# A four-layer graph kernel: loading x first, preparing weights inside the first stage, and starting the second stage while the first ends

## The chip, the cores and the metric

The kernel runs on one core of a Trainium2 chip. The metric is the device time of one execution in microseconds, and lower is better. A core has five engines that run their own instruction streams side by side: TensorE (PE in the profile, its weight loads PEld), VectorE (DVE), ScalarE (ACT), GpSimd (POOL) and SyncE (SP, which here only issues DMAs). ACT and POOL can issue DMAs as well.

## The reference

There are 128 graphs of 128 nodes with 128 channels, and an adjacency matrix (0 or 1) for each graph. Four graph layers follow each other; each normalizes its input, applies a Relu, calls its layer and adds the result to x. The two stages that the change touches compute the first layer:

```python
h = jnp.maximum(_layernorm(x, axis=-1), 0.0)
D = jnp.abs(x[:, :, None, :] - x[:, None, :, :])      # x is h here: all pairs of nodes
h = jnp.einsum('bijc,oc->bijo', D, W1) + b1
m = jnp.mean(h, axis=(0, 1, 2))                        # over all graphs and all pairs
v = jnp.mean((h - m) ** 2, axis=(0, 1, 2))
h = _leaky((h - m) / jnp.sqrt(v + EPS) * g1 + be1)
s = jnp.einsum('bijo,uo->biju', h, W2)[..., 0] + b2[0]
A = jax.nn.softmax(jnp.where(A_init > 0, s, NEG), axis=-1)
y = jnp.einsum('bij,bjc->bic', A, x)                   # then Wg, a second normalization, Wt
```

The mean and the variance need every pair of every graph, while the scores are needed only where the adjacency matrix has an edge. Hence the kernel has two stages for this layer: stage 1 makes the statistics over all pairs, stage 2 the attention on the edges.

## The kernel before

**Preparation (lines 185 to 372).** The kernel builds an identity matrix on POOL, loads some thirty weight arrays (matrices on SP's and ACT's queues, columns such as `b1`, `g1`, `qb`, `vb_c` on POOL's), transposes five square matrices on PE, and folds weights for the later layers: `fw`, `w2g`, `aq`, `vpw`, `pb_bc`, `q_avg` and others. Scratch tiles of the pool `wload` hold the raw weights.

**Stage 1, `statistics()` (lines 484 to 700).** Graphs are taken four at a time, 32 groups. `nodes(g)` loads x (`xg`), normalizes it (DVE statistics `ln_s`, `ln_mv`; ACT `ln_rs`; POOL `ln_xn`), stores it to DRAM (`xn_d`), transposes it on PE (`pt`), applies the Relu (`he`), stores it (`h_d`) and makes three bf16 parts `us` of the product with W1 (`pu`). Then `block(b, q)` runs for every graph and each quarter of its pairs: a difference `d` (128 channels by 2048 pairs) on DVE (line 605) or POOL (line 610), its absolute value on ACT (line 614), a product with W1 on PE (line 631, `ph`), and sums on DVE (line 643) or ACT (line 637). Blocks with `is_larger` take a maximum instead of the difference and add three bf16 products with `us` and a constant pattern `both`. A chain of small operations on DVE, PE and POOL then turns the sums into the scale `h_sc` and the offset `h_bi` (lines 658 to 700).

**Stage 2, `edge_attention()` (lines 702 to 1105).** It first forms constants (`off`, `at`, `in_half`, `in_other`, `not_own`, `upto`, `down`, `least`, `room` and others, lines 716 to 758) and the score of a node with itself (`own`, `own_d`). Then it takes the same 32 groups. A group loads the adjacency matrices (`adj`), `xn` and `ht`, casts to bf16 (`adjb`), ranks the edges (`other`, `half`, `rank`, `keys`, `more`, `ranks`, `pos`, `row`, `in_row`) and so forms a matrix `inc` that selects the edges. For each graph PE then forms the differences over edges (`diff`), ACT takes the absolute value (`d`), PE multiplies by W1 (`ph`), ACT applies the statistics (`z`, with `h_sc` and `h_bi`), and further steps make the scores `pl` and the attention. Side steps split h into bf16 parts (`parts`), form values (`values`, `pz`), check the matrix (`check`, `pc`), form the masked base (`bases`, which needs `own_d`) and store x with a bias (`with_bias`, `xb`).

**What sets the order.** Inside each stage the instruction order of PE, ACT, DVE and POOL is written out by a planner, `in_order`. A step is a generator that yields `(engine, planned work in us, slots it takes, slots it frees)`. Among the steps that are ready the planner takes the one that can begin first. Slots stand for buffers (`p` for PSUM banks, `in` for a group's inputs, `d` for differences), and a chain may wait for a named event with `yield "after", ...`. Each call of the planner starts with all engines free at time 0. SP is not in this order. The kernel's third stage (the remaining layers, from line 1106 on) uses the same planner and is not changed. Stage 2's tiles lie in memory that stage 1 or the weight scratch used before, and stage 1's in that of the weight scratch.

## Time and profile before

| what | value |
|---|---|
| time, median of 3 runs | 2709.62 us (2708.36 to 2710.77) |
| profiled execution: time | 2713.54 us |
| profiled execution: span, first to last instruction | 2711.7 us |
| mean granted TensorE clock | 0.966 |
| first x load issued | 21.49 us |
| first pair block on POOL, DVE | 35.58, 36.08 us |
| POOL's last pair block ends | 1079.9 us |
| first load of stage 2 issued | 1090.17 us |
| first selection product (`diff`) of the steady run | 1115.94 us |

A line of a timeline gives the start, the duration, the engine, the source line, the operation, the tile written and the tiles read, the number of instructions merged into it, and in brackets how long the engine had been idle and what released it. In a table of stretches each engine has its busy time and in brackets its number of instructions. A queue name such as SPq is the time in which an engine issues a DMA. Times of PE are modelled at their ends.

### The profile page before, as it was taken

The numbers are of one execution on the slowest core, as the hardware profiler recorded it, in microseconds if no ns is written. First come the engines' busy times: TensorE is split into PE (matmuls) and PEld (weight loads), VectorE is DVE, ScalarE is ACT, GpSimd is POOL, SyncE is SP. The second block draws the span as 40 slices with busy tenths as digits, with TensorE's granted clock in tenths as the row PEclk, the third lists the DMA queues.
The fourth block names the chain that finished last, engine by engine and source line by source line (L and its number), as shares of the span: only waits on it lengthen the run. The fifth ranks groups of instructions, "written<-read, shape, count | busy, mean of one in ns | idle before, by whom it ended". The sixth has DMA issues, their size and how long they took to land. (4 is left out here: it accounts for less than half of the span.)

```text
span 2711.7 us, 51703 instructions
## 1 busy us (share of the span) xinstructions
PE 2497.3 (92%) x19597; PEld 1559.2 (57%) x19597; DVE 2416.1 (89%) x4660; ACT 2161.6 (80%) x3531; POOL 1644.8 (61%) x943
## 2 busy tenths in 40 slices
PE   6999999999999999799999999968988888898888
PEld 3334333434333333577777777756766767667666
DVE  6999999999999998788988888778988888889886
ACT  4999999999999999466566666568787877787885
POOL 7999999999999999635435343022333333333234
PEclk8999999999999999899999999979999999999999
DMA  2000000000000000523222231040211111111001
GB/s 69 16 27 30 24 24 28 24 24 24 24 24 24 24 20 9 161 74 100 81 85 86 78 100 42 17 137 6 62 29 54 36 44 44 41 42 33 9 2 33
DMA packets 134257, 122.62 MB, mean 45 GB/s; under 512 B 9504, under 2 KB 100960, under 8 KB 134000
## 3 DMA queue, kind: packets, MB, share of 16 engines
q1 hardware_dynamic: 131360, 117.83, 14.1%
q8 instruction: 158, 2.59, 0.4%
q10 hardware_dynamic: 2032, 1.31, 0.2%
q14 instruction: 99, 0.81, 0.1%
q0 software_dynamic: 608, 0.07, 0.0%
HBM read 73.05 MB, written 46.14 MB: 44 GB/s over the span
## 5 line engine op out<-in xcount | busy, mean ns | idle before, releaser
L610 POOL TENSOR_TENSOR d<-he 128x2016 f32<-128x2016 f32 (+1 forms) x272 | 959.8, 3559 | 15.0 <-DVE six L643 7.8
L631 PE MATMUL ph<-d,w1T 128*64 128x504 f32 (+1 forms) x4096 | 910.0, 594 | 22.9 <-DVE six L643 13.2
L614 ACT ACTIVATE d<-d 128x2048 f32<-128x2048 f32 (+1 forms) x448 | 832.2, 1888 | 18.1 <-POOL d L610 12.4
L631 PEld LDWEIGHTS ph<-d,w1T 128*64 128x64 f32 x4096 | 320.2, 136 | 545.0 <-issue 459.9
L605 DVE SCALAR_TENSOR_TENSOR d<-pt,he 128x2048 f32<-128x2048 f32 x240 | 541.4, 2269 | 0.7 <-PE ph L631 0.7
L643 DVE BATCH_NORM_STATS2 six<-ph 128x6 f32<-128x512 f32 (+1 forms) x704 | 435.8, 676 | 13.4 <-PE ph L631 12.0
L1568 POOL TENSOR_TENSOR xn<-xo,mv 128x512 f32<-128x512 f32 x64 | 73.9, 1155 | 324.8 <-DVE mv L1561 257.5
L975 PE MATMUL pl<-its,it 128*128 128x128 f32 x1280 | 168.2, 280 | 1.5 <-DVE its L968 1.2
L875 POOL CAST h<-xn 128x512 bf16<-128x512 f32 x32 | 21.5, 672 | 243.5 <-DVE xn L869 229.4
L637 ACT ACTIVATE ph<-ph 128x1008 f32<-128x1008 f32 x160 | 159.7, 998 | 9.8 <-PE ph L631 8.8
L975 PEld LDWEIGHTS pl<-its,it 128*128 128x128 f32 x1280 | 154.4, 193 | 15.0 <-DVE its L968 6.5
L1671 DVE SCALAR_TENSOR_TENSOR p<-z,mask 128x1024 f32<-128x1024 f32 x124 | 147.7, 1210 | 8.3 <-ACT z L1669 8.0
L1569 POOL TENSOR_TENSOR xn<-xn,rs 128x512 f32<-128x512 f32 x96 | 111.1, 1158 | 49.6 <-ACT rs L1565 37.9
L937 ACT ACTIVATE z<-ph,h_bi,h_sc 128x320 f32<-128x320 f32 x128 | 78.5, 617 | 74.5 <-PE ph L934 73.8
L923 PE MATMUL diff<-inc,h 128*128 128x320 bf16 x768 | 130.0, 306 | 2.9 <-DVE inc L843 2.5
L1669 ACT ACTIVATE z<-z 128x1024 f32<-128x1024 f32 x128 | 129.0, 1008 | 4.0
L930 ACT ACTIVATE d<-diff 128x640 f32<-128x640 f32 x128 | 89.8, 702 | 52.9 <-PE diff L923 51.7
L843 DVE SCALAR_TENSOR_TENSOR inc<-in_row,row 128x4 bf16<-128x4 f32 (+12 forms) x512 | 125.5, 315 | 1.2 <-PE in_row L836 1.2
L965 ACT CAST it<-pi 128x640 f32<-128x640 bf16 x128 | 87.0, 689 | 47.3 <-PE pi L962 46.1
L1568 POOL TENSOR_TENSOR xn<-x,mv 128x512 f32<-128x512 f32 x32 | 36.5, 1139 | 138.3 <-DVE mv L1561 65.9
L968 DVE TENSOR_TENSOR its<-pi,s 128x640 f32<-128x640 bf16 x128 | 102.9, 810 | 15.0 <-ACT it L965 14.1
L1700 PE MATMUL va<-p,vals 128*32 128x128 f32 x2048 | 107.8, 283 | 8.0 <-DVE vals L1685 7.8
(349 smaller groups left out, 5349.8 us busy)
## 6 DMA issues: line engine op xcount, KB each, us to landing
ht<-h SPq DMA_DIRECT2D x64, 256.0 KB, 2.8
xg<-in_x SPq DMA_DIRECT2D x32, 256.0 KB, 2.7
n<-ln_xn SPq DMA_DIRECT2D x32, 256.0 KB, 2.4
h<-he SPq DMA_DIRECT2D x32, 256.0 KB, 2.6
adj<-in_adj SPq DMA_DIRECT2D x32, 256.0 KB, 3.1
xn<-n SPq DMA_DIRECT2D x32, 256.0 KB, 2.7
xb<-in_x SPq DMA_DIRECT2D x32, 256.0 KB, 3.3
xb<-xb SPq DMA_DIRECT2D x32, 256.0 KB, 2.0
```

What stands on the lines that cost most here:

```text
L605: nc.vector.scalar_tensor_tensor(dv, own, 0.0, later, ALU.max, ALU.max if is_larger else ALU.subtract)
L610: nc.gpsimd.tensor_tensor(dv, later, own, ALU.subtract)
L614: nc.scalar.activation(d[:, 0 : 4 * n], d[:, 0 : 4 * n], AF.Abs, accum_out=sums[:, g, k : k + 1] if on_act else None,)
L631: nc.tensor.matmul(ph[64 * a : 64 * a + 64, t, 0:n], wt, x_, start=part == 0, stop=not is_larger or part == 3,)
L637: nc.scalar.activation(ph[:, :, 0:n], ph[:, :, 0:n], AF.Square, accum_out=squares[:, g, k : k + 1])
L643: nc.vector.bn_stats(six[g][:, 2 * by_bn.index((i, q)) + t, :], ph[:, t, 0:n])
L843: nc.vector.scalar_tensor_tensor(inc[:, :, e : e + n], in_row[:, :, 0:n], float(k + 1), row[:, :, 0:n], ALU.is_equal, ALU.subtract,)
L923: nc.tensor.matmul(diff[:, a, 0 : SLOT_N // 2], h[:, i, :], inc[:, a * SLOT_N // 2 : (a + 1) * SLOT_N // 2], start=m == 0, stop=m == 2,)
L975: nc.tensor.matmul(made["pl"][:, i, :], it[:, k, :], its[:, k, :], start=k == 0, stop=k == 4)
L1569: nc.gpsimd.tensor_tensor(xn, xn, bcast(rs, 2, P), ALU.mult)
L1669: nc.scalar.activation(z, z, AF.Exp, scale=1.0 - SLOPE)
L1671: nc.vector.scalar_tensor_tensor(p, z, 1.0, bcast(mask[:, i, :], 1, NH), ALU.max, ALU.mult)
```

## The change

The change has three parts.

1. **Start.** The pools for the later inputs, for stage 2's tiles (`mid`) and for the weight scratch are placed on the other side of the memory. The first two groups of x are loaded there at once, the first as SP's first DMA. All columns that POOL loaded go to SP's queue. POOL's two memsets go to DVE.
2. **Weights inside stage 1.** The preparation becomes generators (`first_weight`, `own_and_later`, `attention_weights`, `square_weights`, `edge_constants`) that the planner of stage 1 places among its own steps, with planned waits of 4 to 30 us ahead of them. `both` is added up on POOL instead of DVE. Four of the transposed matrices are copied together. `edge_constants` holds stage 2's constants; `least` is one instruction instead of 16.
3. **Boundary.** `in_order` returns when each engine and slot is free, and stage 2's call starts from these times. The final statistics become the chain `total`, the first maker of stage 2's planner. A step can wait for several events; two new ones are `begun` (the latest of stage 1's engine times) and `stats` (the end of `total`). Stage 2's inputs and first tiles (`adj`, `xn`, `ht`, `adjb`, `half`, `other`, `more`, `ranks`, `row`, `h1` to `h3`) lie in `mid`, which shares no memory with stage 1's tiles. `z` and the second half of `bases` wait for `stats`; `xb`, `zg`, the first half of `bases`, `inc` and the first `d` wait for `begun`. The two statistics products become one.

```diff
-def in_order(makers, most, room, kept):
+def in_order(makers, most, room, kept, begun=None):
-    free_at = dict.fromkeys(AFTER, 0.0)
-    slots = {kind: [0.0] * n for kind, n in room.items()}
-    chains, events = [], {}
+    free_at = dict.fromkeys(AFTER, 0.0) if begun is None else dict(begun)
+    slots = {kind: [0.0] * n if isinstance(n, int) else list(n) for kind, n in room.items()}
+    chains, events = [], {"begun": max(free_at.values())}
...
+    return free_at, slots
...
+    raw_x = [wl.tile([P, GB, P], F32, tag=f"x{g}", name=f"x{g}") for g in range(2)]
+    nc.sync.dma_start(raw_x[0], x_t[:, 0:GB, :])
...
+    raw("w1", w["L0_gnn_W1"], nc.sync)
+    nc.sync.dma_start(raw_x[1], x_t[:, GB : 2 * GB, :])
...
-        nc.gpsimd.dma_start(t[0:n], src)
+        nc.sync.dma_start(t[0:n], src)
...
+    def attention_weights():
+        yield "wait", 5.0
+        yield DVE, 2.9, "", ""
...
+    def square_weights(psum2):
+        yield "wait", 8.0
+        yield PE, 1.3, "ph", ""
...
+        pt = psum2("w_ps").rearrange("p a (b c) -> p (a b) c", c=P)
+        for k, name in enumerate(("wg", "wt0", "wt1", "kw", "pw")):
+            nc.tensor.transpose(pt[:, k, :], raws[name], ident)
+        yield ACT, 0.9, "", "ph"
...
+        yield PE, 1.7, "ph", ""
+        pv = psum2("vw_ps")
+        pvw, pvb = pv[:, 0, 0:P], pv[0:1, 1, 0:P]
+        nc.tensor.matmul(pvw, raws["vw"], pwT, start=True, stop=True)
+        nc.tensor.matmul(pvb, vb_c, pwT, start=True, stop=True)
...
+    def edge_constants():
+        yield "wait", 30.0
+        yield POOL, 0.6, "", ""
+        nc.gpsimd.iota(
...
+            def own_and_later():
+                yield POOL, 3.9, "", ""
+                nc.gpsimd.tensor_tensor(
+                    both.rearrange("p (i j) -> p i j", j=64),
...
+            def first_weight():
+                yield "wait", 4.0
+                yield PE, 0.3, "ph", ""
...
+                if g < len(raw_x):
+                    xg = raw_x[g]
+                    yield "wait", 4.0 + 1.2 * g
...
-            makers = [partial(nodes, 0)]
+            makers = [partial(nodes, 0), others]
...
+                free_at, slots = in_order(
+                    makers, A_UNDER_WAY + 1, {"d": A_D, "ph": 3} | two, A_KEPT
+                )
+        banks = sorted(slots["pt"]) + [at for at in sorted(slots["ph"]) for _ in range(2)]
+
+        def total(psum, done):
+            yield "after", "begun"
+            yield DVE, 1.0, "", ""
...
+            yield "done", "stats"
...
             def bases(g, adjb, made):
+                yield "after", "begun"
                 yield ACT, 0.62, "", ""
                 base = tile_f("base")
                 nc.scalar.activation(base, adjb, AF.Identity, bias=far, scale=-NEG)
+                yield "after", "stats"
                 yield POOL, 2.5, "", ""
...
+                if g == i == 0:
+                    yield "after", "begun"
                 yield ACT, 0.6, "d", "q"
...
+                yield "after", "stats"
                 yield ACT, 0.53, "", "p"
                 z = made["z"][:, i, :]
...
-            makers = [partial(group, g) for g in range(n_parts)]
+            makers = [partial(total, psum, own_d), *(partial(group, g) for g in range(n_parts))]
```

## The prediction

> **What bounds the kernel now.** I read the page's first two parts, then a table of busy time by stage, then the timelines at both places the change touches. Columns of a stage row: stretch, its length, busy time and instruction count of PE, PEld, DVE, ACT, POOL, granted clock, DMA share, GB/s.
>
> ```profile
> span 2711.7 us, 51703 instructions
> PE 2497.3 (92%) x19597; PEld 1559.2 (57%) x19597; DVE 2416.1 (89%) x4660; ACT 2161.6 (80%) x3531; POOL 1644.8 (61%) x943
> ...
> 0.00:36.00 36.00, 14.31 (x56) 9.65 (x56) 16.24 (x71) 7.59 (x21) 18.75 (x36) 0.78 0.40 111
> 36.00:1090.00 1054.00, 1031.78 (x5224) 412.67 (x5224) 1033.63 (x1279) 1025.18 (x1075) 1026.30 (x360) 1.00 0.07 23
> 1090.00:1116.00 26.00, 10.63 (x62) 8.45 (x61) 19.57 (x108) 7.21 (x14) 18.12 (x19) 0.73 0.69 214
> 1116.00:1774.00 658.00, 626.12 (x5428) 484.41 (x5427) 549.18 (x1413) 403.68 (x853) 267.08 (x242) 0.97 0.24 77
> ```
>
> The reader should see four stretches with different limits. In the first 36 us no engine is half busy beyond POOL: weights are prepared and nothing of x is worked on. From 36 to 1090 (stage 1) four engines are all 97 to 98% busy, DVE the fullest: no engine has room for much more. From 1090 to 1116 PE works 10.6 of 26 us, partly at half clock. From 1116 PE carries stage 2 (626 of 658 us).
>
> The timeline of the start and of the boundary (start, duration, engine, line, operation, idle before and its releaser):
>
> ```profile
> 6.88 1.28 ACT L494 ACT_TABLE_LOAD   x1 [6.88 <-DMA a2b<-in_L_gnn_a]
> 21.49 6.49 SPq L525 DMA_DIRECT2D xg<-in_x  x3
> 21.87 2.29 DVE L512 TENSOR_TENSOR both<-ident 128x2048 bf16<-128x2048 f32 x1
> 35.58 42.24 POOL L610 TENSOR_TENSOR d<-he 128x2016 f32<-128x2016 f32 x12
> 36.08 2.28 DVE L605 SCALAR_TENSOR_TENSOR d<-pt,he 128x2048 f32<-128x2048 f32 x1
> ```
>
> ```profile
> 1090.17 0.39 SPq L793 DMA_DIRECT2D adj<-in_adj  x1
> 1093.35 0.61 POOL L802 CAST adjb<-adj 128x512 bf16<-128x512 int32 x1 [13.46 <-DMA adj<-in_adj]
> 1095.22 0.22 DVE L437 SCALAR_TENSOR_TENSOR h_bi<-af_off,h_sc,be 128x1 f32<-128x1 f32 x1
> 1110.73 0.40 PE L836 MATMUL in_row<-row,ranks 128*128 128x128 bf16 x4 [3.71 <-DVE row L832]
> 1115.94 1.49 PE L923 MATMUL diff<-inc,h 128*128 128x320 bf16 x5 [2.47 <-DVE inc L843]
> ```
>
> The first x load is issued only at 21.49, after the last use of the weight scratch, and the first pair block follows 14 us later. At the boundary POOL, done with stage 1 at 1079.9, idles 13.46 us for a load that is issued at 1090.17, when stage 1's memory comes free. The statistics are ready at 1095.2, but PE gets its first diff at 1116: the long chain there is group 0's own (load, adjb, half, rank, row, inc).
>
> **The start, part by part.** x is issued at about 0.7 in place of 21.49 and needs 2.8 us to land, so about 4. Its four statistics took 2.2 us (24.25 to 26.4): 6.2. Next is ACT's rs, behind the table load, which stood at 6.88 because ACT first issues seven DMAs. Those paused: a2b was issued at 3.71, when w1c had landed (0.74 plus 3.0), and araw at 5.55, when Wg had (1.38 plus 4.1): as if some eight transfers could be under way at once. The change puts 19 small DMAs of POOL on SP, so that SP issues 27 (0.37 to 0.59 us each, 10 to 16 us) and with ACT's 34 share that limit: 34 / 8 x 3.5 us is 15 us. So the table load ends between 8.2 (as now) and 15; I take 10.5, nearer the row because ACT's issues are early in each queue. Then rs 0.5, product on POOL 1.04, transposes 1.11, Relu 0.60, copy 0.40 and hand-overs: he is whole at about 14.4. POOL's second normalization (2.1) comes next: its first d at 16.5 instead of 35.58, 19 us earlier. DVE's first d waits for pu and the three us parts (1.8 + 4 x 0.42 and hand-overs): 18.5 instead of 36.08, 17.5 earlier. PE follows at 20.8 instead of 38.42, 17.6 earlier. A DMA store of xn or h behind SP's 27 issues delays no one: its buffer is wanted a group, 33 us, later. SP's late ones are vb_c and pb_row: PE's pvb and DVE's sum wait for them (12 to 16 plus 2.3 us to land), and behind them on PE stands pu of group 0: 0 to 4 us, inside my range.
>
> The forming of "both" moves from DVE (2.29) to POOL; the nearest POOL row is a 2016-element difference at 3.56. It ends near 5 to 6, before POOL's first wanted product at 10.5: it costs nothing. [...]
>
> **What is now inside stage 1.** From the rows before 22 us and at 1095 to 1099, DVE's moved work is: layer 1's attention weights 6.4 (products 0.76 and 0.84, sums 0.74 twice, copies 0.74, ident_far and the small sums 1.9, the rest of it 0.7 and hand-overs), square weights 2.2 (aT 1.08 in it), stage 2's constants 5.4, sign of both and w1T2 0.9: 14.9 us. Some 4 fit before the first d; 11 stand between pair blocks, and the third group's statistics (1.6), formerly before 36, too. Hence DVE nets 17.5 - 12.6 = 5 us. PE has 30 instructions, 7 us, most before its first block: nets 15. POOL loses 2.1 and 0.5 for the iotas: nets 16. ACT loses 2.5: nets 15. If DVE carries the stage strictly, it ends 5 us earlier (0 if the start is at its late bound); if PE does, 15. Against DVE as the only limit: from 1050 to 1089 PE never stopped, and DVE's idle time in the last 20 us of it was about 8, waiting for ph. I take 9, bounds 0 and 16.
>
> **The boundary.** Stage 1 ends on PE at T = 1089.9; the first diff is at T + 26. Now three groups' adj, xn and ht lie in memory of their own, loaded before; POOL goes on at T - 10 with adjb 0.6, other and half 2.75, so rank can run right at T. DVE then has for group 0: keys and more 0.9, ranks, pos, row 3.3, parts 0.8, inc 3.9: 8.9 us, with PE twice between (1 us), and the statistics' DVE steps (7.6 planned; 1088.8 to 1095.2 measured, waits included) woven in; about 3 us of theirs stand in group 0's way. First diff at T + 13: 13 us saved. Bounds: 6, if all statistics go ahead of group 0; 18, if they fall into its gaps. Constants (5.4 on DVE, done at 1099.2) leave this path; they were paid above. New waits: z on ACT, and base plus edge on POOL, wait for the statistics (own_d, some T + 12). Behind z on ACT stand other groups' copies, and ph keeps a bank: but first ph comes about T + 14, so the wait has ended. d of graph 0 and the xb load wait for "begun", which is T + 1: nothing.
>
> PE's clock fell to 0.50 between 1095 and 1105 and again between 1115 and 1120; 24 pz matmuls took 5.41 us there. PE still has gaps in my sum, so I count no gain from it; full clock would give about 3. [...]
>
> **Sum.** 9 + 13 = 22 us from the profiled execution: 2713.54 (span 2711.7, 1.8 around it) gives 2691.5. That execution was 3.9 above the median 2709.62, so I expect 2687.6, say 2688. Within 0.2% (5.4 us) this kernel can't be told from no change.
>
> **Rivals.** *DVE carries all of it.* Late table load and 12.6 us of DVE work eat the start; only the boundary remains, at 6 to 13: 2709.6 - 10 = 2700. For it: DVE is the fullest engine, 98.1%. Against: the PE tail.
> *Both ends do better.* DVE's slack absorbs the inserts (15 to 16) and the boundary gives 18, or a warm clock 3 more: 35 saved, 2675. For it: POOL, ACT and PE all start 17 to 19 earlier.
> *Stage 2 runs worse (the slower side).* Its whole order is planned anew, from unequal free times and with new waits. The place is the 658 us from 1116; PE is busy 95.2% of it. Each point of that share costs 7 us; the 22 us are gone at 626 / 680 = 92.1%, and at 91% (688 us) the time is 2718. For it: the planner's plan doesn't hold on the chip exactly; after 1774 PE is busy only 814.5 of 938. Against: nine groups are under way and PE's waits in stage 2 are single microseconds per line.
> *It doesn't do what it says:* stage 2 loads still wait for stage 1, the start gains 4 to 8: 2703.
>
> **How the numbers follow.** Forecast 0.62 (2678 to 2699), DVE 0.13, better 0.13, worse 0.09, doesn't 0.03. Leaving out the far halves of the outer cases, 8 in 10 is 2673 to 2706. Faster by over 0.2% (under 2704.2): 0.62 + 0.13 + 0.11 + 0.01 = 0.87; within: 0.05; slower: 0.08.
>
> **What would show it.** Right: the first POOL d near 16 and PE's first block near 21; last stage 1 matmul near 1081 (1076 to 1090); first diff 8 to 20 us after it; POOL casts adjb directly after its last d, not after a DMA; stage 2 still about 655 us. Wrong: ACT's table load after 15; PE waiting for vb_c beyond 20; DVE idle under 3 us in the last 40 us of stage 1 (DVE carries); diff still 25 us behind stage 1; PE under 93% in stage 2.

## The result: 28 us slower, and where the time is

Before and after were run side by side, five times each. The changed kernel takes 2737.26 us (2736.23 to 2743.38) and the kernel before 2709.13 us (2708.36 to 2710.77). The ratio is 1.0109, with a 95% interval of 1.0095 to 1.0124. The prediction was 2688. The profiled execution of the changed kernel took 2736.81 us, with a span of 2735.0.

The stages show that the loss and a gain partly cancel. All times are from the two profiled executions, in us.

| place in the profile | before | after | change |
|---|---|---|---|
| first pair block on POOL (`d`) | 35.6 | 37.4 | +1.8 |
| first pair block on DVE (`d`) | 36.1 | 53.9 | +17.8 |
| first stage 1 product on PE (`ph`) | 38.4 | 56.3 | +17.9 |
| last stage 1 product begins | 1089.5 | 1140.5 | +51.0 |
| first `diff` of stage 2 | 1113.0 | 1159.9 | +46.9 |
| last `diff` of stage 2 | 1745.2 | 1770.6 | +25.4 |
| span | 2711.7 | 2735.0 | +23.3 |

So the first 56 us lose 18, the rest of stage 1 loses another 33 (1084.2 us from the first product to the last, 1051.1 before), the boundary gains 4 (19.4 us from the last product to the first diff, 23.5 before), and stage 2 gains 21.5 (610.7 us from the first to the last diff, 632.2 before). What follows the last diff is 2 us shorter. (The ratios are worked out from the single runs, so they can differ a little from the quotient of two medians. The first `diff` of the table is a single product; the steady run begins at 1115.94 before and at 1162.69 after.)

The page of the changed kernel, first part, and then the table of busy time by stretch (columns as in the table of before: PE, PEld, DVE, ACT, POOL, granted clock, DMA share, GB/s):

```profile
span 2735.0 us, 51581 instructions
PE 2485.0 (91%) x19595; PEld 1552.3 (57%) x19595; DVE 2456.2 (90%) x4648; ACT 2159.1 (79%) x3527; POOL 1634.4 (60%) x923
...
0.00:56.00 56.00, 8.97 (x36) 7.28 (x36) 29.31 (x71) 8.55 (x20) 28.53 (x24) 1.00 0.49 139
56.00:1141.00 1085.00, 1041.45 (x5244) 417.85 (x5245) 1052.79 (x1308) 1024.66 (x1075) 1020.63 (x362) 0.99 0.07 22
1141.00:1163.00 22.00, 9.07 (x72) 6.77 (x71) 17.01 (x64) 7.03 (x15) 9.58 (x10) 0.76 0.50 155
1163.00:1799.00 636.00, 614.84 (x5415) 480.12 (x5413) 559.64 (x1415) 399.89 (x849) 261.07 (x241) 0.98 0.24 77
```

DVE is busy 40 us longer over the whole kernel (2456.2 against 2416.1) with 12 instructions fewer, and 19 us longer in stage 1 alone (1052.79 against 1033.63). PE, by contrast, is busy 12 us less (2485.0 against 2497.3). The timeline of the changed kernel's start shows both halves of the loss:

```profile
19.80 0.98 SPq L617 DMA_DIRECT2D xg<-in_x  x2
...
24.29 0.29 DVE L622 BATCH_NORM_STATS2 ln_s<-xg 128x6 f32<-128x128 f32 x1 [13.84 <-DMA xg<-in_x]
...
25.90 0.26 DVE L622 BATCH_NORM_STATS2 ln_s<-x 128x6 f32<-128x128 f32 x1
...
38.24 2.94 DVE L339 COPY w2g<-gw 128x2 f32<-128x2 f32 x1
...
45.18 3.31 DVE L341 TENSOR_SCALAR ident_far<-ident 128x128 bf16<-128x128 f32 x1
...
49.32 2.62 DVE L355 TENSOR_TENSOR parts_m<-of_part 128x1 f32<-128x1 f32 x1
...
53.89 2.22 DVE L700 SCALAR_TENSOR_TENSOR d<-pt,he 128x2048 f32<-128x2048 f32 x1
...
26.06 1.04 POOL L631 TENSOR_TENSOR ln_xn<-xg,ln_mv 128x512 f32<-128x512 f32 x1 [21.07 <-DVE ln_mv L623]
...
37.42 14.49 POOL L705 TENSOR_TENSOR d<-he 128x2016 f32<-128x2016 f32 x4
```

The first half is a wait in DVE's order. The first two groups of x (tile `x`) were issued at 0.74 and 1.87 us, but DVE takes the statistics of the third group (tile `xg`) first. That load is an ordinary one, and SP issues it at 19.80, behind 27 others. DVE stands idle for 13.84 us until it lands, and everything else it has to do, the first two groups' statistics at 25.90 and the weights included, stands behind.

The second half is the duration of small operations. POOL's first four differences begin at 37.42 and, one by one, end at 41.15, 44.91, 48.41 and 51.92. A copy of 128x2 that took 0.16 us before begins at 38.24 and ends at 41.18; `ident_far`, 0.22 us before, ends at 48.49; a sum of two columns, 0.16 us before, ends at 51.94. Each ends just after a POOL difference has ended. Between 31 and 130 us, twelve lines of the weights' preparation with 16 such operations add up to 32.7 us. Where POOL does next to no arithmetic, as in the preparation of the kernel before, the same work takes 3.9 us. The difference is 29 us of DVE time that no plan had. Some 12 of these 29 us stand before DVE's first difference and are part of the late start.

The boundary in the timeline of the changed kernel:

```profile
1125.29 15.77 PE L726 MATMUL ph<-d,w1T 128*64 128x512 f32 x72
1142.32 0.38 PE L886 MATMUL rank<-upto,other 128*128 128x128 bf16 x4 [1.26 <-ACT ph L732]
1143.17 0.69 DVE L893 TENSOR_TENSOR more<-key_row,keys 128x512 bf16<-128x512 f32 x1 [0.21 <-PE key_row L888]
...
1145.90 0.28 PE L776 MATMUL act_m<-all_sums,w1TT 128*128 128x1 f32 x2
...
1150.28 0.68 DVE L899 TENSOR_TENSOR ranks<-rank,half 128x512 bf16<-128x512 f32 x1
...
1152.34 0.56 PE L907 MATMUL in_row<-row,ranks 128*128 128x128 bf16 x4 [0.73 <-DVE row L903]
...
1157.28 0.22 DVE L518 SCALAR_TENSOR_TENSOR h_bi<-af_off,h_sc,be 128x1 f32<-128x1 f32 x1
...
1157.61 1.28 DVE L916 SCALAR_TENSOR_TENSOR inc<-in_row,row 128x512 bf16<-128x512 f32 x2
...
1162.69 1.49 PE L1000 MATMUL diff<-inc,h 128*128 128x320 bf16 x5 [2.40 <-DVE inc L916]
```

The loads are indeed out of the way: `rank` runs 1.3 us after stage 1's last product, which ends at T = 1141.06. But between `more` (done at 1143.9) and `ranks` (1150.28) DVE works on the statistics, and waits 1.76 us in it for their first product, which PE does only after a group of `pz` and `pc`. After `in_row` (done at 1152.9) DVE finishes all the statistics, 1157.5, before it takes `inc`. The steady run of diffs begins at T + 21.6; before it was T + 26.

Stage 2 itself was not expected to move. The kernel before has gaps in it that the changed one does not have. Two stretches of 5 us of before (columns as above), and the matmul in them:

```profile
1305.00:1310.00 5.00, 3.21 (x20) 2.08 (x21) 4.32 (x8) 0.96 (x5) 4.92 (x5) 0.67 0.01 2
1310.00:1315.00 5.00, 5.00 (x39) 3.33 (x38) 2.79 (x5) 3.27 (x8) 0.76 (x2) 0.65 0.79 238
```

```profile
1307.33 1.02 PE L943 MATMUL sp<-w_slide,z 128*128 128x2 f32 x4 [1.79 <-DVE z L448]
```

PE waits 1.79 us for DVE, and the granted clock in these 10 us is 0.67 and 0.65. In narrower stretches it is 0.50 from 1306.7 to 1313.4, where PE is busy 6.07 us. Six `diff` products took 0.99 us at 1302.14, at a clock of 1.00, and 1.78 us at 1309.85, at 0.50; by that ratio some 3 us of work are lost beside the gap, an estimate. The clock falls to 0.50 in the same way near 1487.6 (6.7 us), 1654.9 (3.3) and 1678.8 (3.3). The whole hundreds of microseconds around them have PE busy 95.3 to 98.7 us at a clock of 0.97 to 1.00. In the changed kernel, from 1262 on, each hundred has 98.7 to 99.1 us at 1.00. The waits of PE in stage 2, by cause, fall from 18.5 us to 7.4, and PE's busy time there from 626 to 615 us for the same work. Together that is about the 21 us.

### The profile page after: what moved, and what is told of

Read it like the earlier page. It is cut to its first block, busy times and chain, and to the rows that moved or that the text cites. A ratio compares the mean times of both kernels' runs of the same rounds, so it can differ in the third digit from the quotient of the medians.

```text
span 2735.0 us, 51581 instructions
## 1 busy us (share of the span) xinstructions
PE 2485.0 (91%) x19595; PEld 1552.3 (57%) x19595; DVE 2456.2 (90%) x4648; ACT 2159.1 (79%) x3527; POOL 1634.4 (60%) x923
## 4 chain that ended last, share of the span: by engine, by line
PE 43%; DVE 34%; ACT 12%; issue 6%; POOL 3%; DMA 1%; SPq 0%; DVEq 0%; ACTq 0%; POOLq 0%
PE ph L726 12%; DVE d L700 8%; DVE six L738 6%; ACT d L709 4%; PE pl L1055 4%; PE diff L1000 4%; DVE p L1751 3%; PE ph L1013 2%; POOL d L705 2%; PE sp L1023 2%; PE po L1708 2%; PE va L1780 1%; DVE s L1639 1%; ACT ph L732 1%; PE ph L1910 1%
## 5 line engine op out<-in xcount | busy, mean ns | idle before, releaser
L726 PE MATMUL ph<-d,w1T 128*64 128x512 f32 (+1 forms) x4096 | 914.5, 597 | 43.4 <-DVE six L738 29.8
L709 ACT ACTIVATE d<-d 128x2016 f32<-128x2016 f32 (+1 forms) x448 | 831.0, 1887 | 38.6 <-DVE d L700 23.7
L987 POOL TENSOR_TENSOR base<-base,own_d 128x512 f32<-128x512 f32 x32 | 42.7, 1334 | 177.5 <-PE ph L1013 121.5
L916 DVE SCALAR_TENSOR_TENSOR inc<-in_row,row 128x8 bf16<-128x8 f32 (+12 forms) x512 | 126.5, 315 | 0.8 <-PE in_row L907 0.8
L1996 POOL TENSOR_TENSOR xh<-xh,xo 128x512 f32<-128x512 f32 x32 | 46.9, 1468 | 106.0 <-DVE xh L1717 82.2
```

The source lines that it names most:

```text
L709: nc.scalar.activation(d[:, 0 : 4 * n], d[:, 0 : 4 * n], AF.Abs, accum_out=sums[:, g, k : k + 1] if on_act else None,)
L726: nc.tensor.matmul(ph[64 * a : 64 * a + 64, t, 0:n], wt, x_, start=part == 0, stop=not is_larger or part == 3,)
L916: nc.vector.scalar_tensor_tensor(inc[:, :, e : e + n], in_row[:, :, 0:n], float(k + 1), row[:, :, 0:n], ALU.is_equal, ALU.subtract,)
```

## The experiments

The theory after the result: **(1)** the late third load makes DVE and all behind it start late; **(2)** small DVE operations beside POOL's differences last until the running difference ends; **(3)** stage 2 gains from its new order. Rivals: the loss is the new weight work as such, or the order of stage 1; and stage 2 gains from its own memory, not the order. This table has, from each profiled execution, the start of DVE's first `d`, the time from the first to the last stage 1 product, from there to the first diff, and from the first to the last diff. The ratio is to runs of the kernel before on the same chip, whose medians were 2712.89 (e1 to e4), 2711.6 (e5 to e8) and 2710.02 us (e9 to e11).

| kernel | time, us | ratio, 95% interval | DVE's first `d` | stage 1 | to diff | diffs |
|---|---|---|---|---|---|---|
| before | 2709.13 | 1 | 36.1 | 1051.1 | 23.5 | 632.2 |
| after | 2737.26 | 1.0109 (1.0095 to 1.0124) | 53.9 | 1084.2 | 19.4 | 610.7 |
| e1 three x | 2714.84 | 1.0001 (0.9991 to 1.0011) | 36.1 | 1075.0 | 19.4 | 610.9 |
| e2 three x, weights first | 2689.00 | 0.9909 (0.9893 to 0.9926) | 31.0 | 1054.7 | 19.4 | 611.0 |
| e3 boundary alone | 2690.55 | 0.9909 (0.9893 to 0.9926) | 32.1 | 1054.5 | 19.4 | 612.1 |
| e5 planned from zero | 2706.13 | 0.9975 (0.9966 to 0.9985) | 32.7 | 1051.6 | 23.7 | 623.2 |
| e7 one order | 2698.67 | 0.9957 (0.9940 to 0.9974) | 44.6 | 1051.5 | 19.4 | 610.8 |
| e8 weights, then pairs | 2704.73 | 0.9979 (0.9968 to 0.9989) | 35.3 | 1070.7 | 19.5 | 611.7 |
| e9 the same, one order | 2695.35 | 0.9948 (0.9931 to 0.9964) | 26.0 | 1069.1 | 19.4 | 613.0 |
| e10 order alone | 2703.02 | 0.9972 (0.9961 to 0.9982) | 38.2 | 1050.5 | 23.7 | 619.4 |
| e11 two x, weights first | 2715.96 | 1.0024 (1.0014 to 1.0033) | 37.9 | 1074.4 | 19.5 | 613.3 |

### e1: a third group of x loaded early

```diff
-    raw_x = [wl.tile([P, GB, P], F32, tag=f"x{g}", name=f"x{g}") for g in range(2)]
+    raw_x = [wl.tile([P, GB, P], F32, tag=f"x{g}", name=f"x{g}") for g in range(3)]
...
-    nc.sync.dma_start(raw_x[1], x_t[:, GB : 2 * GB, :])
+    for g in (1, 2):
+        nc.sync.dma_start(raw_x[g], x_t[:, g * GB : g * GB + GB, :])
```

> Edit: the changed kernel with a third group of x in the early loads, so that DVE's first statistics no longer stand behind an x load that SP issues after 24 small ones. Theory A (DVE's head-of-line wait until 24.3 us cost about 18 us of the start, the rest is lost elsewhere): POOL's first pair block near 18 to 22 us in place of 37.4, time 2737 - 15 to 20 = about 2719. Rival B (the weight steps on DVE set the start and the wait lies beside them): POOL's block moves, but DVE's first pair block and the time do not, 2733 to 2739.

Measured: 2714.84 us, 22 below the changed kernel, with DVE's first difference at 36.1; POOL's came at 27.9 and not at 18 to 22. In the profile the last stage 1 product comes 27 us earlier, 18 of them from the start and 9 from the stage, and what follows the last diff took 6 us longer in this execution. Set against the kernel before on its own chip, the difference is 26. The late load is worth 22 to 27 us by itself. What remains above the boundary's gain is stage 1, still 24 us longer than before's. In it DVE is idle for almost nothing in the first 100 us; the small operations fill it: those that begin after DVE's first difference take 23 us. From the groups of DVE by shape between 36 and 130 us of e1 (count, busy us, mean ns, idle before):

```profile
L397 DVE COPY aT<-araw 128x256 f32<-128x256 f32 x4 | 4.6, 1148 | 0.0
L437 DVE TENSOR_SCALAR back<-at 128x128 f32<-128x128 f32 x1 | 3.6, 3637 | 0.0
L438 DVE TENSOR_TENSOR tmp<-back,ident 128x128 f32<-128x128 f32 x1 | 3.5, 3534 | 0.0
```

Other lines are hit than in the changed kernel (there `back` took 1.2 us and `tmp` 1.1), as is to be expected if chance decides at what point of a POOL difference an operation begins. The trace of e1 also shows the wait that the prediction put at 0 to 4 us: PE stands 8.11 us before `pvb`, until 23.07, for `vb_c`, with the first group's `pu` behind it.

### e2: the same, and the weights ahead of everything

```diff
-                if g == 0:
-                    yield "after", "w1"
-                    yield "after", "both"
...
-            makers = [partial(nodes, 0), others]
+            makers = [partial(nodes, 0)]
...
+            for gen in (own_and_later(), first_weight(), attention_weights(), square_weights(psum2), edge_constants()):
+                for _ in gen:
+                    pass
             with tc.manual_schedule(engines=ORDERED):
...
-                    makers, A_UNDER_WAY + 1, {"d": A_D, "ph": 3} | two, A_KEPT
+                    makers, A_UNDER_WAY, {"d": A_D, "ph": 3} | two, A_KEPT
```

The chain of the weights no longer counts among those under way, so their number goes down by one.

> Edit: as the first run, and all weight and constant steps taken out of the planner's order, ahead of stage 1. Theory C (DVE copies and scalar operations that run beside a POOL pair block last 1 to 3.6 us instead of 0.2, about 30 us in all, and this is what moving them into stage 1 cost): no weight operation over 1.3 us, last pair product of stage 1 near 1085, time 2685 to 2695. Rival D (their own length is the cost, 11 us, wherever they stand): 2705 to 2712.

Measured: 2689.00 us, 26 below e1, 0.9% below the kernel before and 1.8% below the changed one. No weight operation stands in stage 1, and the stage is back to 1054.7 us. DVE even begins its pair blocks 5 us earlier than in e1, because the same operations are short while POOL has no pair blocks (`a1bc` and the scaling of `pb_row` took 3.32 and 3.08 us in e1, 0.73 and 0.31 here).

### e3: the boundary and stage 2 alone

The weights stand ahead of stage 1 as in e2, all 19 column loads are on POOL's queue again, and no x is loaded early.

```diff
-    raw_x = [wl.tile([P, GB, P], F32, tag=f"x{g}", name=f"x{g}") for g in range(2)]
+    raw_x = [wl.tile([P, GB, P], F32, tag=f"x{g}", name=f"x{g}") for g in range(0)]
...
-    nc.sync.dma_start(raw_x[1], x_t[:, GB : 2 * GB, :])
...
-        nc.sync.dma_start(t[0:n], src)
+        nc.gpsimd.dma_start(t[0:n], src)
```

> Edit: the changed boundary and second stage, but weights prepared ahead of stage 1, columns loaded by POOL as before, and no x load ahead of the weights. If the boundary and the newly planned stage 2 are worth what the profile of the changed kernel shows (4 us to the first diff, 21 us inside stage 2), and stage 1 starts and runs as before or a little earlier: 2680 to 2688. If stage 2 was only faster because stage 1 ended late or left something done: 2700 to 2710.

Measured: 2690.55 us, just above the range for the gain standing by itself. The first product on PE comes 4 us earlier than in the kernel before (x no longer shares memory with the weight scratch). The rest of the gain is the boundary (4) and stage 2 (20), less 3 in stage 1. So the early x, which was the first part of the change, is worth next to nothing against e3: e2, which has three early groups, is 1.6 us below it, within the spread.

### e4: small operations in stage 1 of the kernel before

```diff
+            def probe(k):
+                yield DVE, 0.3, "", ""
+                kind = k % 4
+                if kind == 0:
+                    nc.vector.tensor_copy(pr_a, ident)
+                elif kind == 1:
+                    nc.vector.scalar_tensor_tensor(pr_b, ident, 1.0, ident_h, ALU.mult, ALU.max)
+                elif kind == 2:
+                    nc.vector.tensor_reduce(pr_c, ident, AX.X, ALU.add)
+                else:
+                    nc.vector.tensor_scalar(pr_b, ident, 2.0, None, ALU.mult)
...
+                if 4 <= b < 124:
+                    makers.append(partial(probe, b))
```

> Edit: the kernel before, with 120 small DVE operations on 128x128 in stage 1, 30 each of: copy f32 to bf16, scalar_tensor_tensor with two inputs, reduction, scalar operation f32 to f32. They add work that nothing uses. Theory C: copies and scalar operations last 1.5 to 2 us on average beside POOL's pair blocks (each waits for the running one), with single values up to 3.6; the reduction and the two-input operation 0.3 to 0.4; the time grows by 80 to 130 us. Rival D: all four last 0.2 to 0.4, time at most 40 us longer.

Measured: one time of 2892.01 us, 179 above the kernel before and so more than the 80 to 130 of theory C. The groups of DVE by shape:

```profile
L656 DVE SCALAR_TENSOR_TENSOR pr_b<-ident,ident_h 128x128 f32<-128x128 f32 x30 | 76.9, 2562 | 0.0
L660 DVE TENSOR_SCALAR pr_b<-ident 128x128 f32<-128x128 f32 x30 | 55.7, 1857 | 0.0
L654 DVE CAST pr_a<-ident 128x128 bf16<-128x128 f32 x30 | 44.8, 1493 | 0.0
L658 DVE TENSOR_REDUCE pr_c<-ident 128x1 f32<-128x128 f32 x30 | 7.9, 265 | 0.0
```

120 operations that the plan held to be 0.3 us each take 185 us, and the time grows by 179: in stage 1, DVE time is time. The sums stay at 0.265 us, the other three kinds do not. That the two-input kind would stay short was wrong: it was the longest.

### e5: the boundary alone, but planned from zero

```diff
-                    makers, B_GROUPS, {"p": banks[0:6], "q": banks[6:7], "in": B_IN, "w": B_W, "d": 3, "it": 3, "ge": 1, "eT": 2, "yt": 2, "xb": 2}, {"p": 1}, free_at
+                    makers, B_GROUPS, {"p": 6, "q": 1, "in": B_IN, "w": B_W, "d": 3, "it": 3, "ge": 1, "eT": 2, "yt": 2, "xb": 2}, {"p": 1}
```

> The kernel of the boundary alone, with stage 2's planner called as before the change: every engine and slot free at time 0. Memory, tiles, constants, loads and the chain of the statistics stay as changed. Theory A (the 21 us of stage 2 come from the new order, since the planner now knows when each engine comes free): the stretch from the first to the last diff goes back from 611 to about 632 us, PE again shows gaps of 1 to 2 us with a granted clock near 0.6 behind each, and the time is 2690.5 + 21 = 2711. Theory B (they come from the memory of their own and the loads made ahead, not from the order): the stretch stays at 609 to 615 and the time within 5 us of 2690.5.

Measured: 2706.13 us, between the theories. The diffs take 623.2 us, 11 of the 21 are back, and the boundary is 23.7 us as in the kernel before. The waits of PE and its clock come back too (100 us stretches at 0.95 to 1.00). So with the other parts in place, knowing when each engine comes free is worth about 16 us in all: 4 at the boundary and 11 in stage 2. The rest of stage 2's gain needs something else as well; see e10.

### e6: what lengthens a small operation

A call of `round_of` runs the eight kinds on DVE, with 2 to 8 sums after each; the copy of `last` makes the second set wait until POOL is done.

```diff
+            for r in range(14):
+                round_of(r, True)
+            for _ in range(115):
+                nc.gpsimd.tensor_tensor(big_o, big_a, big_b, ALU.subtract)
...
+            nc.vector.tensor_copy(last, big_o[:, 0:1])
+            for r in range(14):
+                round_of(r, True)
```

> The kernel before, with a stretch put ahead of stage 1 whose results nothing uses: POOL runs 115 differences of 128x2016 (3.56 us each) while DVE runs eight kinds of small operations on 128x128, 14 of each, with 2 to 8 small sums between them; then DVE runs the same list again with POOL idle. Theory A (a DVE operation that reads and writes SBUF, whatever its number of inputs, waits for POOL's running operation; one that reads PSUM, a sum and a memset do not): in the first stretch copy, one-input and two-input kinds have means of 1 to 2.5 us and none above about 3.9, the PSUM kinds, sums and memsets stay at 0.17 to 0.45; in the second stretch all stay at 0.16 to 0.45. Theory B (any DVE operation beside POOL is slowed by a share): all kinds are longer in the first stretch by the same factor. Theory C (the lengthening has to do with stage 1's other work on ACT and PE, not with POOL): no kind is longer in the first stretch. The time is some 600 to 900 us above before's; nothing is read from it.

Groups of DVE by shape while POOL works:

```profile
L1130 DVE TENSOR_REDUCE o_sum<-src 128x1 f32<-128x128 f32 x560 | 158.8, 284 | 15.5
L1116 DVE TENSOR_TENSOR o_two<-src,ident 128x128 f32<-128x128 f32 x14 | 44.5, 3176 | 0.0
L1115 DVE TENSOR_SCALAR o_one<-src 128x128 f32<-128x128 f32 x14 | 43.5, 3106 | 0.0
L1114 DVE COPY o_copy<-src 128x128 f32<-128x128 f32 x14 | 34.2, 2443 | 0.0
L1120 DVE TENSOR_SCALAR o_h<-src_h 128x128 bf16<-128x128 bf16 x14 | 31.8, 2270 | 0.0
L1117 DVE SCALAR_TENSOR_TENSOR o_ps<-ps_in,src 128x128 f32<-128x128 f32 x14 | 3.9, 281 | 0.0
L1122 DVE SCALAR_TENSOR_TENSOR o_max<-ps_in,ident 128x128 f32<-128x128 f32 x14 | 3.9, 281 | 0.0
```

and the same list with POOL idle:

```profile
L1130 DVE TENSOR_REDUCE o_sum<-src 128x1 f32<-128x128 f32 x560 | 159.2, 284 | 15.5
L1116 DVE TENSOR_TENSOR o_two<-src,ident 128x128 f32<-128x128 f32 x14 | 3.9, 282 | 0.0
L1117 DVE SCALAR_TENSOR_TENSOR o_ps<-ps_in,src 128x128 f32<-128x128 f32 x14 | 3.9, 281 | 0.0
L1114 DVE COPY o_copy<-src 128x128 f32<-128x128 f32 x14 | 3.0, 217 | 0.0
L1115 DVE TENSOR_SCALAR o_one<-src 128x128 f32<-128x128 f32 x14 | 3.0, 216 | 0.0
```

Theory A holds, with longer means than it named. Copies, one-input and two-input operations between tiles in SBUF go from 0.18 to 0.28 us up to means of 2.27 to 3.18 us, the longest 4.38, which is about the length of one POOL operation here (4.43 us; 3.56 in stage 1; why the two differ was not tested). Operations that read PSUM (0.281 us), memsets (0.165) and sums over a row (0.284) do not change at all. POOL's own 115 operations all last 4.42 to 4.46 us, whether DVE works beside them or has already finished its first set. PE and ACT had nothing to do in either stretch, which excludes theory C. Stage 1's own DVE work consists of the kinds that are spared: `d` (2.27 to 2.28 us in every trace here) and the operations that make `us` (0.41) read PSUM, and the rest are statistics, which in the kernel before last as long beside POOL's differences as with POOL idle (`six` 0.68 and 0.69 us, `ln_s` 0.26 in both). That is why stage 1 of the kernel before shows nothing of this, and why the weights, most of them SBUF to SBUF, met it as soon as they were moved there. The boundary of the kernel before does show it, beside POOL's products there:

```profile
1101.03 1.17 DVE L776 TENSOR_SCALAR own_d<-ident,own_c 128x128 f32<-128x128 f32 x1
1108.97 1.70 DVE L832 TENSOR_TENSOR row<-at,pos 128x512 bf16<-128x512 f32 x1
```

The same two take 0.29 us (at 1158.98) and 0.69 us (at 1151.59) in the changed kernel. The prediction counted the 1.70 as `row`'s own length.

What holds these operations up inside the core no run shows. The lists show which kinds are held up: with two inputs in SBUF (`o_two`) 3.18 us in place of 0.28, with one input in SBUF (`o_one`) 3.11 in place of 0.22, and with one of two inputs in PSUM (`o_ps`, `o_max`) 0.281 both times. Beside POOL's unbroken row, the kinds that wait last 11 to 14 times their own duration. The other direction is in the changed kernel: POOL's first two differences begin beside a `prod` of DVE with two SBUF inputs, and they take 3.73 and 3.79 us in place of 3.56.

### e7: one order round both stages

```diff
-            with tc.manual_schedule(engines=ORDERED):
-                free_at, slots = in_order(
...
+            free_at, slots = in_order(
...
-    edge_attention(*statistics())
+    with tc.manual_schedule(engines=ORDERED):
+        edge_attention(*statistics())
```

> The kernel with the weights ahead of stage 1 and three early x loads, with one written-out order round both stages, so that POOL's casts and products of stage 2's first three groups can't come ahead of stage 1's pair blocks. Theory A (those 8.8 us of POOL work among the blocks cost nothing there, since DVE sets stage 1's end): the end of stage 1 moves by under 3 us and, since the casts and products now follow POOL's last difference, the first diff comes 0 to 6 us later: 2686 to 2695. Theory B (POOL's share counts as well): the end of stage 1 is 6 to 9 us earlier and the time about 2681 to 2684.

Measured: 2698.67 us, outside both ranges, because the one order also put the first groups' normalization behind all the weights: DVE's first difference is at 44.6, 13.6 us later than in e2. The stage itself answers the question. It takes 1051.5 us against e2's 1054.7, and the boundary stays at 19.4, so POOL's early casts and products for stage 2 cost 3 us where they stand among the pair blocks and save nothing there. (e5, in which POOL's products for stage 2 also come after the stage, has 1051.6.) With e2's start, 13.6 us earlier, and the same stage, its time would be about 2685, an estimate; that combination was not run.

### e8 and e9: the weights in the planner's order, but ahead of the pair blocks

Beside three early groups of x, `vb_c`, `pb_row`, `acol` and `qb` become SP's first columns, ACT's table load goes ahead of its DMAs, and the planned wait of the constants goes from 30 to 3 us.

```diff
                 yield "fork", edge_constants()
                 yield "join",
+                yield "done", "weights"
...
                     yield "after", ("nodes", g)
+                    if g == 0:
+                        yield "after", "weights"
```

> The changed kernel with three early x loads, whose planner may not begin a pair block before the weights are done, with vb_c, pb_row, acol and qb as the first of the columns on SP and with ACT's table load ahead of its DMAs. The weights stay in the planner's order, beside the first groups' normalization. Theory A (the cost of the weights inside stage 1 is that of DVE operations beside POOL's pair blocks, and the rest of it the order behind late loads): no weight operation of 128x128 is above 0.5 us, the first difference on DVE comes at 25 to 30 us (31.0 with the weights ahead of everything), and the time is 2683 to 2689. Theory B (in the planner's order the weights wait for late columns and hold up DVE and PE whatever is done): the first difference on DVE comes after 33 and the time is above 2691.

Measured: 2704.73 us, as theory B had it. Even with the table load at 0.73 us, ACT's first operation comes at 11.41, behind its own DMA issues (qw at 9.08, vw at 11.04), and with it everything that waits for ACT. POOL's first difference started at 24.88 while DVE still had weights to do, and `a1bc` took 3.44 us beside it.

e9 mends these: qw and vw go to SP, planned waits are set to the landings seen, and one order is put round both stages.

> An attempt at a better start: planned order for weights and normalization with pair blocks only after the weights; three early x loads; vb_c, pb_row and acol right behind them on SP; qw and vw on SP too, so that ACT is done issuing at about 5 us; planned waits of the weights set to the landings in the earlier traces (6.5 and 13 us); one written-out order round both stages. Theory A (the start was held up by ACT's issues and late columns): first difference on DVE at 24 to 29 us, stage 1 in 1051 us, first diff at 1095 to 1103, time 2674 to 2684. Theory B (SP's queue now makes something else late that stands ahead in the order): first difference on DVE after 31, time 2688 or more.

Measured: 2695.35 us. The first difference on DVE came at 26.0, as theory A had it, but stage 1 took 1069.1 us and not 1051, and so the time missed by 11 us. Of the weights only one copy of 0.16 us (`aqb`) stands in the stage. From the groups of DVE in e9's stage 1, by shape:

```profile
L741 DVE BATCH_NORM_STATS2 six<-ph 128x6 f32<-128x512 f32 x510 | 320.9, 685 | 20.3 <-PE ph L729 19.7
```

DVE waits for products of PE. It is the same in e11, next.

### e11: two early groups of x, weights first

Against e2 only the early loads are different:

```diff
-    raw_x = [wl.tile([P, GB, P], F32, tag=f"x{g}", name=f"x{g}") for g in range(3)]
+    raw_x = [wl.tile([P, GB, P], F32, tag=f"x{g}", name=f"x{g}") for g in range(2)]
...
-    for g in (1, 2):
-        nc.sync.dma_start(raw_x[g], x_t[:, g * GB : g * GB + GB, :])
+    nc.sync.dma_start(raw_x[1], x_t[:, GB : 2 * GB, :])
```

> The changed kernel with the weights' and constants' steps ahead of the planner's order, as in the fast kernel before, but with only two groups of x loaded early, as changed. It tells whether the 22 us of the late third group stand by themselves. Theory A (DVE waits for the third group's load whatever else it has to do): about 2689 + 22 = 2711. Theory B (the wait was dear because the first group's statistics and the weights stood behind it; with the weights ahead DVE has work until the load lands): 2687 to 2696, first difference on DVE at 31 to 36 us.

Measured: 2715.96 us, 27 above e2 (31 by the ratios), near theory A's number but not by its mechanism alone. DVE waited only 2.43 us for the third load, and its pair blocks began 6.9 us later than e2's. The other 20 us are inside stage 1 (1074.4 against 1054.7), in which not one weight operation stands. The waits of DVE in stage 1 (cause, us in total, times, longest), for e11 and then for e2:

```profile
DVE six L735 <- PE ph L723: 30.4, 34, 3.9
DVE pu L654 <- ACT us L652: 8.2, 4, 6.8
```

```profile
DVE six L736 <- PE ph L724: 13.7, 26, 3.3
```

DVE is as busy in the stage as in e2 (1034.6 against 1033.7 us), so all of it is waiting. The reading here is that each engine meets the others' work at the wrong moments when a load is late or another group comes first, until all four are full again at about 215 us: between 40 and 215 us DVE is busy 151.6 us in e11 and 171.2 in e2. No run isolates this. The waits for `ph` are 12 to 15 us in the runs whose stage 1 was planned as in the kernel before (before, e2, e3, e7) and in e1, and 22 to 30 in the changed kernel, e8, e9 and e11. The clock can have a share in it. In e11 the granted clock is 0.90 from 50 to 100 us, by which PE lost at most about 5 us of work there (0.10 of 50, an estimate). In the changed kernel, e1, e8 and e9 it is 0.86 to 0.90 in the same 50 us, while in the other kernels of the table it is 1.00, or 0.98 in e7. From 100 to 1050 us it is 1.00 in all of them.

### e10: stage 2's order alone

This is the kernel before with the changed `in_order`, which hands the times at which engines and banks come free to stage 2's call.

```diff
-                    makers, B_GROUPS, {"p": 6, "q": 1, "in": B_IN, "w": B_W, "d": 3, "it": 3, "ge": 1, "eT": 2, "yt": 2, "xb": 2}, {"p": 1}
+                    makers, B_GROUPS, {"p": banks[0:6], "q": banks[6:7], "in": B_IN, "w": B_W, "d": 3, "it": 3, "ge": 1, "eT": 2, "yt": 2, "xb": 2}, {"p": 1}, free_at
...
-    statistics()
-    edge_attention()
+    edge_attention(*statistics())
```

> The kernel before with one thing of the change: stage 2's planner starts from the times at which stage 1's planner left each engine and bank free. Memory, loads, constants, the chain of the statistics and the start stay as before. Theory A (the gain in stage 2 is the order alone): from the first to the last diff 609 to 618 us in place of 632, and a time about 15 to 22 us below before's. Theory B (it needs the other parts too, the memory of their own above all): 625 to 635 us, and a time within 7 us of before's.

Measured: 2703.02 us, 7 below the kernel before, and 619.4 us for the diffs, just outside theory A's range; the time is at the edge of theory B's. The two parts of stage 2's gain can now be set beside each other, in us from the first to the last diff: neither 632.2, the known times alone 619.4 (-13), the rest alone (e5) 623.2 (-9), both 610.7 to 613.3 (about -20). They add up within a few us. With the times alone, the largest wait of PE in stage 2 is 11.4 us for `inc`; in e3 there is no such wait. What follows the last diff in this stage is 3 us longer in e5 and e10 than in the kernel before (30.4 against 27.1 us), and the time shows less than the diffs for that reason. Which of the other parts (memory, early loads, the constants moved away) makes the 9 us was not separated.

## Why the prediction was wrong

**"Its four statistics took 2.2 us: 6.2"** failed first. x landed in time (at the latest 6.6 us after its issues at 0.74 and 1.87), but the step took for granted that DVE does the first group first. The planner gave the third group's ordinary load a planned 0.6 + 2.2 us and the early groups a planned wait of 4.0, so the third group came first in DVE's order, and on SP its load stood behind 27 issues. The prediction named SP's queue and looked at stores and at `vb_c` in it, but not at this load, although it counted the third group's statistics. Price: 22 to 27 us (e1). The first difference on POOL came at 37.4 and not 16.5, on DVE at 53.9 and not 18.5.

**"14.9 us ... 11 stand between pair blocks"** failed by its durations. They were taken from stretches in which POOL did next to no arithmetic. From 29 us on, beside POOL, the same work is 41.6 us of DVE (12.7 of it own duration, 29 waiting for POOL's operation). e4 and e6 measured the price, and e2 took it away: 26 us with the start it delayed.

**"DVE carries the stage strictly ... 5 us earlier, 0 at the late bound"** failed in its bounds: 0 and 16 us saved left no room for a loss, and the last stage 1 product came 51 us later. It also assumed that DVE waits no more in the stage than before. DVE's busy and idle time, from its first difference to the stage's end, splits the cost:

| kernel | stretch, us | length | DVE busy | DVE idle |
|---|---|---|---|---|
| before | 36 to 1090 | 1054 | 1033.6 | 20.4 |
| after | 54 to 1141 | 1087 | 1054.8 | 32.2 |
| e1 | 36 to 1114 | 1078 | 1054.5 | 23.5 |
| e2 | 31 to 1089 | 1058 | 1033.7 | 24.3 |
| e11 | 38 to 1115 | 1077 | 1034.6 | 42.4 |

Of the 33 us in the changed kernel 21 are work and 12 waiting. The work is the weights: those that begin after DVE's first difference take 22 us. In e1, 21 of the 24 us are work and 3 waiting; e2 waits as long as e1, so the 20 us between their stages are the work alone and not the one chain fewer. In e11 there is no such work, and all of the loss is waiting.

**"I take 10.5" for the table load, "0 to 4" for `vb_c`:** the table load ended at 9.96, near enough. The wait for `vb_c` was 8.1 us in e1, and in the changed kernel it is hidden by the larger ones.

**"POOL ... both ... costs nothing"** held: it took 3.60 us from 1.4 to 5.0, as the row of 3.56 said.

**"First diff at T + 13: 13 us saved. Bounds: 6"** failed: 4.4. The mechanism was right (no load in the way, POOL's products ready, `rank` at T + 1.3), but "about 3 us" of statistics in group 0's way were all of them, twice: ahead of `ranks` (6.4 us) and ahead of `inc` (4.7 us). The bound was too narrow because it counted DVE's operations and not its waits for PE between them. For the clock the prediction counted no gain, since PE still had gaps; that gaps hold the clock down was its author's estimate, and no run isolates it. The granted clock was 0.76 in the 22 us from 1141 to 1163 of the changed kernel and 0.73 in the 26 us from 1090 to 1116 of the kernel before.

**"Stage 2 still about 655 us"** failed to the other side: 636. The rival that spoke of the new order saw only a loss in it. The rows for the gain were in the profile of before: PE's waits of 18.5 us and the clock of 0.97 in four of the six full hundreds from 1116 on hold more than 20 us of room, which the prediction read as "single microseconds per line".

**The rivals.** The slower side had the right sign and the wrong place. "DVE carries all of it" had the right engine, and its reason, the fullest engine gets more work, was enough for a loss once the price of that work was right.

## What to carry to other kernels

Before moving small operations beside a GpSimd that works without a break, sort them by where they read and write: here copies and one- or two-input operations that stay in SBUF took 1.5 to 3.2 us on average (e4, e6), 0.4 to 0.7 of a GpSimd instruction of 3.56 or 4.43 us, while those that read PSUM (0.28 us), row sums (0.26 to 0.28) and memsets (0.165) took their own time. In a written-out order, follow the first instruction of each engine back to the queue that issues its load, since one late load in front cost more here (22 us or more, e1) than all the early ones gained (1.6, e2 against e3). And when a stage's order is planned, plan it from the times at which engines really come free: that was worth about 16 us here with the rest of the boundary in place (e5 against e3), and 7 by itself (e10). The version to keep is e2 (or e3): new boundary and order, weights ahead of stage 1, 2689.00 us.

## What was unexpected in the hardware

A DVE copy of two elements per partition lasted 2.94 us beside a POOL difference of 3.73 us, and 0.16 us alone; a 128x128 operation two differences later lasted 3.31. The length followed the end of POOL's instruction, not the size: they ended at 41.18 and 48.49, POOL's differences at 41.15 and 48.41. POOL hardly pays: its operations last 4.42 to 4.46 us in e6, with DVE beside it and without, though 3.73 and 3.79 in place of 3.56 where DVE's operation had begun first.

PE's clock fell to 0.50 four times in stage 2 of the kernel before, for at least 6.7, 6.7, 3.3 and 3.3 us. The longest gaps of PE just before were 1.79, 1.79, 2.15 and 0.30 us, while one of 2.26 us, up to 1191.80, left the clock at 1.00. So the length of the gap alone did not decide it here. Small `sp` products (128x2 and 64x1) stand within 5 us before each fall; whether they matter is not shown.

SP issues a tiny column load in 0.33 to 0.60 us, and the set of 19 of them took from 8.85 to 19.75 us in the changed kernel. These 10.9 us are longer than the wait for the largest load of the preparation: the 512 KB of `araw` landed 4.7 us after its issue in the kernel before.
